# A conditioned two-layer transformer on one core: the order of a bias on GpSimd, the order of products at a stage's junction, and the slots of side work

## The chip, the core and the metric

The kernel runs on one core of a Trainium2 chip. A core has five engines with instruction streams of their own: TensorE (PE in the profile) multiplies matrices, VectorE (DVE) and GpSimd (POOL) do elementwise work and reductions, ScalarE (ACT) does elementwise functions, SyncE (SP) issues most of the DMA transfers. The metric is the time of one execution in microseconds (us). The kernel before took 1510.19, 1506.1 and 1509.9 us in three runs, a median of 1509.9 us.

## What is computed

x has 32 batches of 128 tokens with 512 features. Layer 0 acts on groups of four batches (512 tokens), with 16 heads; layer 1 acts on each batch's 128 tokens with a single head. Every batch also has a condition vector, from which the scales and shifts come.

```python
# layer 0 (h: the input; gamma, beta from the condition)
def sln(h):   # layer norm, then gamma * ln + beta
    mu, var = mean(h), mean((h - mu) ** 2)
    return gamma * ((h - mu) / sqrt(var + 1e-5) * ln_g + ln_b) + beta
q, k, v = split_heads(sln(h) @ Wqkv.T + bqkv)          # 16 heads of 32
out = softmax(q @ k.T) / sqrt(512) @ v
h1  = out @ Wp.T + bp + h
x   = sln(h1) + h1

# layer 1 (rmsnorm, then x * (1 + scale) + shift, both from the condition)
a = film(rmsnorm(x, norm1_w))
out = softmax((a @ q_w + q_b) @ (a @ k_w + k_b).T * 512 ** -0.5) @ (a @ v_w + v_b)
x = x + out @ proj_w + proj_b
m = film(rmsnorm(x, norm2_w))
x = x + gelu(m @ mlp_w1 + mlp_b1) @ mlp_w2 + mlp_b2     # 512 -> 2048 -> 512, exact gelu
```

## The kernel before

**Precision.** A factor is held as two parts, high (rounded to the matmul's fp32r type) and low (what is left). A product is the sum of three matmuls, high by high, high by low and low by high (mm3, L148). So wherever a factor is made there are an ACT cast for the high part and a subtraction for the low part, on VectorE or POOL.

**Order.** Nearly everything lies in two scheduled blocks in which PE, VectorE, ACT and POOL execute in the order of the program text; only SP's DMA queue is put in order by a scheduler. So the order of calls in the Python text is the order of each engine's queue: an instruction that waits holds back everything behind it on its engine. A product's instructions go to PE where `run(...)` stands; what follows it (`done`, an add or a cast) goes to its engine's queue at that place too. PSUM tiles for products have two buffers (mm_tile), so a product can begin only when what was in the tile two before has been read.

**Stages.** After a prologue, **loop one** (L1252 to L1320) has 32 steps s, a chunk of four heads of a group in each: energies, maxima, exponentials and heads_out of step s, the query and key products of step s+1, the layer norm of a later batch (`new`, class Turned), and the output projection of a batch whose heads are done (`end`, class End). An End loads x again (tile xe), adds the projection's bias on POOL (bias, L610), adds the product on VectorE (add, L625), takes the second sln's statistics (first: L296 to L301, the power on POOL L308, L639, L640 on POOL) and ends in second (L644 and a store). A Turned has the steps stats (VectorE L296 to L301 or L306, then the power -0.5 on POOL, L308, whose result is rn), norm (VectorE L374 in layer 0; L372 and L377 in layer 1), halves (ACT L386 and a transposing DMA), merge (VectorE L395), rest (ACT L412, L421) and low (L425, on POOL in layer 1).

The **junction** (L1331 to L1351) leads from layer 0 to layer 1. It is a list of eleven products of twelve matmuls each: K[1..3], the remaining keys of layer 1's group 0 (K[0] stands in loop one's last step); the numbers 0 to 3, the last four Ends, each with its bias on POOL before and its add behind, but with first and second put off to layer 1; and V[0..3], the values. Between them a Pipeline makes the normalised batches of the next group; at u=2 the low part (POOL L425) of the first of them is made.

**Layer 1's attention** (L1360 to L1400) runs over g = 0 to 6. A g scores and softmaxes group g (scores1, softmax1 with L756 on POOL and L759 to L762 on VectorE) and then has eight slots u. A slot runs one key or value product of group g+1 (V has its low part on VectorE, L123); beside it stand the division of the softmax (divided1, L775 and L776) at u=0, its transposes (turn1, tile psaT) at u=1, and the output products of group g (class Out: a load of xe, a bias on POOL L798 at u=2 to 5, product and add L805 at u=3 to 6). The put-off Ends have first at u=2 and second at u=4 of g=0 to 3.

Two kinds of MLP work are spread over these slots. **Tokens** are the first eight batches' second norm (Turned(2, b)): `at` names the slot (g, u) at which each begins with stats; its load comes two slots earlier, norm and halves one slot later, merge and rest six later, and rest ends in a store (hTd). **Columns** (L872) are the four columns i of the first half MLP's right-hand factors x, u, v, y: each loads two stored tokens (b = i and 4 + i), forms sums on VectorE (L890 to L893), high parts on ACT (heads) and low parts (tails, L909) one slot later, x and u on POOL, v and y on VectorE. Before, sums stand at u = 1, 2, 4, 6 of g=6 and a column is loaded one slot ahead.

The passage **g=7** (L1403 to L1425) has no next group; the first seven MLP products, hidden(0, 0), are put between the last scores, transposes and output products. Then **layer2** runs the MLP four times (n = 0 to 3), with columns for n = 1 to 3 inside.

Of the kernel before, what the change touches and what calls it, by code (L numbers as in the profile page):

```python
# [22 lines left out]
G = 4  # L23
NG = B // G
# [17 lines left out]
def cond_seq_kernel(ctx: ExitStack, tc, x, condT, wcond, w0, w1, wk1, wm1, wm2, cols, rows, out):  # L42
    nc = tc.nc
# [822 lines left out]
    def a_load(n, h):  # L866

        t = w_tile(f"A{n}{'hl'[h]}").rearrange("p c f -> p (c f)")[:, : NA * 2 * P]
        load(t.bitcast(FP), ad[n % FH, h])
        At.setdefault(n, []).append(t.rearrange("p (c k f) -> p c k f", c=NA, k=2))  # L870

    class Columns:  # L872
# [9 lines left out]
        def sums(self):  # L882
            n, i = self.n, self.i
            if i == 0:
                Bt[n] = [w_pair(f"B{n}{nm}") for nm in "xuv"]
                t = w_tile(f"B{n}y")
                Bt[n].append((t[:, :2], t[:, 2:]))
            r1, r2 = self.r
            t = d_tile(f"T{n}_{i}", FP, (P, 2 * KC, P))
            nc.vector.tensor_tensor(t[:, 0:2], r2[:, :2], r1[:, :2], ALU.subtract)  # L890
            nc.vector.tensor_tensor(t[:, 2:4], r2[:, 2:], r2[:, :2], ALU.subtract)
            nc.vector.tensor_tensor(t[:, 4:6], r2[:, 2:], t[:, 0:2], ALU.subtract)
            nc.vector.tensor_tensor(t[:, 6:8], t[:, 4:6], r1[:, 2:], ALU.subtract)  # L893
            self.parts = [
                (*(p[:, :, ts(i, P)] for p in pair), src, eng)
                for pair, src, eng in zip(
                    Bt[n],
                    (r1, t[:, :4], t[:, 4:], r2[:, 2:]),
                    (nc.gpsimd, nc.gpsimd, nc.vector, nc.vector),
                )  # L900
            ]

# [346 lines left out]
    with tc.manual_schedule(engines=ordered):  # L1249
        new, end = coming(0), None  # L1250
        staged = None
        for s in range(STEPS):  # L1252
# [4 lines left out]
                ready = None  # L1257
            if ready:
                ready.merge()
            if end:  # L1260
                end.bias()
            run(q)
            if s == STEPS - 1:
                staged()
# [6 lines left out]
            if new:  # L1271
                new.stats()
                new.norm()
            if ready:
                ready.low()
            if end:
# [26 lines left out]
            if s == STEPS - 1:  # L1303
                K = keys1(0)
# [24 lines left out]
        for slot in (-11, -10):  # L1329
            pipe.made[slot] = begins[slot]()  # L1330
        V = values1(0)  # L1331
        products = [K[1], K[2], 0, K[3], 1, V[0], 2, V[1], 3, V[2], V[3]]
        for u, stream in enumerate(products):
            pipe.start(u - 11)
            if u == 1:
# [15 lines left out]
            pipe.end(u - 11)  # L1351


        at = [(1, 5), (2, 5), (3, 5), (4, 1), (4, 5), (5, 1), (5, 3), (5, 5)]
        batches = [0, 1, 4, 5, 2, 6, 3, 7]
        columns, COLUMNS = {}, (1, 2, 4, 6)
        tokens = Pipeline(
            {2 * G * g + u: lambda b=b: Turned(2, b) for (g, u), b in zip(at, batches)}
        )
        for g in range(NG - 1):  # L1360
# [4 lines left out]
            for u in range(2 * G):  # L1365
                slot = 2 * G * g + u
                for line in (pipe, tokens):
                    line.start(slot)
                if u - 1 in columns:
                    columns[u - 1].tails()  # L1370
                if u in columns:
                    columns[u].sums()
                if 0 < u <= G:
                    outs.append(Out(g * G + u - 1))
                late = ends[g] if g < G else None
# [14 lines left out]
                    run(outs[u - 3].stream())  # L1390
                for line in (pipe, tokens):
                    line.end(slot)
                if u in columns:
                    columns[u].heads()
                if g == NG - 2:
                    if u + 1 in COLUMNS:
                        columns[u + 1] = Columns(0, COLUMNS.index(u + 1))
                    if u == 6:
                        for h in range(2):
                            a_load(0, h)  # L1400


        g = NG - 1  # L1403
# [8 lines left out]
        for j in range(3):  # L1412
            run(products[j])
        divided1(g)
        run(products[3])
        turn1(g)
        for o in outs:
            o.bias()
        run(products[4])
        for f in (0, FH):  # L1420
            wb_piece(f)
        for i, o in enumerate(outs):
            run(o.stream())
            if i < 2:
                run(products[5 + i])  # L1425
        row2 = load(r_tile("row2"), rows[R_B2].partition_broadcast(P))
        for q in (1, 3):
            wb_load(q)
# [74 lines left out]
```

## Time and profile before

The profile is of one execution on the chip, recorded by the hardware profiler.

| what | us |
|---|---|
| median of three runs | 1509.9 |
| the profiled execution | 1510.46 |
| its span in the trace | 1508.5 |
| loop one, 32 steps | 54 to 597 |
| junction, first key product to layer 1's first scores | 592.72 to 626.97 |
| layer 1, starts of g = 0 to 6 | 626.97, 656.23, 685.72, 716.23, 746.75, 776.57, 805.23 |
| passage g=7 | 841.60 to 861.35 |
| MLP | to 1508 |

The mean clock granted to TensorE was 0.993 of full speed. How to read it: times in the trace are microseconds from the span's start, and an instruction is named by its line and its output tile. The span is the time between the first and the last record; the execution is 2.0 us longer. A busy time counts the time in which an instruction is under way on its engine, including time in which it is held back while it runs. Before each instruction the trace gives the engine's idle time and the engine that ended it. Stages overlap, as the other engines work ahead of or behind TensorE; the boundaries in the table are TensorE's.

### The profile page before, as it was taken

Reading aid. Unit: us, or ns where it says so; the run is one execution under the profiler, and the core shown is the slowest. Engines: PE = TensorE matmul, PEld = TensorE weight load, DVE = VectorE, ACT = ScalarE, POOL = GpSimd, SP = SyncE. Lnnn points to the kernel's source line nnn. Section 1 sums busy time; section 2 is a strip of 40 time slices with the busy share of each in tenths; the row PEclk is TensorE's granted clock in tenths of the full one; section 3 lists DMA queues with packets and bytes.
Section 4 is the critical chain, followed back from the end, with each engine's and each line's share of the span. In section 5 each row is a group of like instructions: output and inputs, shape, how many; then the busy total and the mean of one; then the engine's idle time right before and its main releaser. Section 6 shows DMA issues by size and latency. Waiting matters only on the chain.

```text
span 1508.5 us, 25450 instructions
## 1 busy us (share of the span) xinstructions
PE 1478.3 (98%) x9612; PEld 1155.3 (77%) x9612; DVE 1008.4 (67%) x1793; ACT 760.5 (50%) x1415; POOL 499.5 (33%) x440
## 2 busy tenths in 40 slices
PE   8999999999999999999999899999999999999998
PEld 3767776777777766787887788888888888888887
DVE  4656777777777667889997776665557555754342
ACT  1455655566555444666786354535454345523331
POOL 1213554445453243466555422230014000340000
PEclk9999999999999999999999999999999999999999
DMA  8245465664655335788885877937776666934550
GB/s 312 85 151 157 125 198 176 188 190 134 178 152 175 111 115 178 193 209 225 233 214 173 356 238 236 307 132 209 225 266 208 194 203 219 326 122 134 184 173 29
DMA packets 226578, 287.85 MB, mean 191 GB/s; under 512 B 107252, under 2 KB 138100, under 8 KB 224024
## 3 DMA queue, kind: packets, MB, share of 16 engines
q1 hardware_dynamic: 225448, 278.89, 59.8%
q10 hardware_dynamic: 1008, 7.34, 1.4%
q8 instruction: 75, 1.23, 0.3%
q14 instruction: 47, 0.39, 0.1%
HBM read 194.23 MB, written 72.55 MB: 177 GB/s over the span
## 4 chain that ended last, share of the span: by engine, by line
PE 81%; DVE 11%; ACT 3%; issue 2%; POOL 1%; DMA 1%; SPq 0%; POOLq 0%; DVEq 0%; ACTq 0%
PE acc L981 23%; PE psh L157 20%; PE psk L157 6%; PE psv L157 5%; PE psq L157 5%; PE psp L157 5%; PE psV L157 2%; PE pse L526 2%; PE pst L561 2%; PE pso L581 2%; PE pss L586 2%; PE psT L157 1%; DVE tn L395 1%; PE pss L747 1%; DVE stn L296 1%
## 5 line engine op out<-in xcount | busy, mean ns | idle before, releaser
L308 POOL TENSOR_TENSOR rn<-vn,neghalf 128x1 f32<-128x1 f32 x96 | 61.6, 642 | 438.9 <-DVE vn L306 336.6
L386 ACT COPY tn<-x 128x1024 uint16<-128x1024 uint16 x90 | 94.0, 1045 | 60.5 <-DVE x L372 48.4
L919 ACT ACTIVATE c<-c,col 128x512 f32<-128x512 f32 x64 | 46.4, 725 | 141.2 <-DVE c L944 86.0
L538 DVE TENSOR_REDUCE nm<-pse 128x4 f32<-128x512 f32 x128 | 79.4, 682 | 19.4 <-PE pse L526 19.4
L997 POOL TENSOR_TENSOR xe<-xe,row 128x512 f32<-128x512 f32 x32 | 46.5, 1484 | 123.8 <-DMA xe<-xs 123.7
L934 DVE TENSOR_TENSOR c<-psh,ca 128x512 f32<-128x512 f32 x32 | 22.1, 692 | 89.9 <-PE psh L157 84.3
L395 DVE COPY tn<-tn 128x1024 uint16<-128x1024 uint16 x90 | 77.0, 855 | 1.0 <-DMA tn<-tn 1.0
L644 DVE SCALAR_TENSOR_TENSOR xe<-te,re,xe 128x512 f32<-128x512 f32 x28 | 41.1, 1467 | 47.4 <-POOL xe L640 47.4
L296 DVE BATCH_NORM_STATS2 stn<-x 128x6 f32<-128x512 f32 x96 | 65.4, 682 | 5.3 <-DMA x<-in_x 5.2
L568 ACT ACTIVATE e<-pst 128x512 f32<-128x512 f32 x128 | 65.8, 599 | 2.6 <-PE pst L561 2.5
L412 ACT ACTIVATE tn<-tn,mods 128x128 f32<-128x128 f32 x128 | 52.5, 481 | 19.0 <-DVE tn L395 19.0
L308 POOL TENSOR_TENSOR re<-ve,neghalf 128x1 f32<-128x1 f32 x32 | 30.9, 966 | 88.7 <-DVE ve L301 88.7
L372 DVE TENSOR_SCALAR x<-x,rn 128x512 f32<-128x512 f32 x64 | 52.9, 827 | 10.1 <-POOL rn L308 9.0
L610 POOL TENSOR_TENSOR xe<-xe,row 128x512 f32<-128x512 f32 x32 | 42.3, 1323 | 47.7 <-DMA xe<-in_x 46.8
L509 ACT ACTIVATE qk<-psq,col 128x512 f32<-128x512 f32 x32 | 22.1, 690 | 69.7 <-PE psq L157 63.5
L947 DVE TENSOR_TENSOR ca<-psh,ca 128x512 f32<-128x512 f32 x32 | 22.1, 691 | 41.5 <-PE psh L157 41.5
L561 PE MATMUL pst<-qk 32*128 32x128 f32 x1024 | 46.2, 295 | 0.0
L798 POOL TENSOR_TENSOR xe<-xe,row 128x512 f32<-128x512 f32 x32 | 45.8, 1444 | 1.1 <-DMA xe<-xs 1.1
L919 ACT ACTIVATE cb<-cb,col 128x512 f32<-128x512 f32 x32 | 23.2, 725 | 43.1 <-DVE cb L948 43.1
L526 PEld LDWEIGHTS pse<-qk 32*128 32x128 f32 x1024 | 32.1, 186 | 14.2 <-issue 12.7
L412 ACT ACTIVATE tn<-tn,mod 128x128 f32<-128x128 f32 x104 | 42.9, 485 | 0.0
L593 DVE TENSOR_TENSOR pss<-pss,rs 128x512 f32<-128x512 f32 x32 | 22.3, 697 | 29.9 <-ACT rs L592 29.8
(1388 smaller groups left out, 4846.5 us busy)
## 6 DMA issues: line engine op xcount, KB each, us to landing
mod<-mod SPq DMA_DIRECT2D x34, 512.0 KB, 5.4
x<-xs SPq DMA_DIRECT2D x64, 256.0 KB, 3.8
xe<-xs SPq DMA_DIRECT2D x64, 256.0 KB, 3.2
ur<-ud SPq DMA_DIRECT2D x64, 256.0 KB, 4.2
xs<-xe SPq DMA_DIRECT2D x60, 256.0 KB, 2.6
x<-in_x SPq DMA_DIRECT2D x32, 256.0 KB, 3.8
xe<-in_x SPq DMA_DIRECT2D x32, 256.0 KB, 4.3
scw<-scw SPq DMA_DIRECT2D x32, 256.0 KB, 4.7
```

What stands on the lines that cost most here:

```text
L157: nc.tensor.matmul(st["ps"], *calls[j], start=(j == 0), stop=(j == n - 1))
L296: nc.vector.bn_stats(st, t)
L308: nc.gpsimd.tensor_tensor(r, v, neghalf, ALU.pow)
L386: nc.scalar.copy(halves.rearrange("p (e d) -> p e d", e=2), X.bitcast(U16).rearrange("p (d e) -> p e d", e=2),)
L395: nc.vector.tensor_copy(self.a.bitcast(U16).rearrange("p (f e) -> p e f", e=2), self.t.bitcast(U16).rearrange("p (e f) -> p e f", e=2),)
L412: nc.scalar.activation(dst[:, c], self.a[:, ts(c, P)], AF.Identity, bias=m[:, q + B : q + B + 1], scale=m[:, q : q + 1],)
L526: nc.tensor.matmul(banks[r][:, ts(i, P)], q[32 * r : 32 * r + 32, ts(i, P)], k[32 * r : 32 * r + 32, ts(i, P)], start=True, stop=True,)
L538: nc.vector.tensor_reduce(nm[:, r], chunks(banks[r]), AX.X, ALU.max, negate=True)
L561: nc.tensor.matmul(banks[r][:, ts(i, P)], k[rr, ts(i, P)], q[rr, ts(i, P)], start=False, stop=True,)
L568: nc.scalar.activation(e, banks[r], AF.Exp)
L919: nc.scalar.activation(t[nm], t[nm], AF.Gelu, bias=col[:, C_B1 + f : C_B1 + f + 1], scale=1.0)
L981: nc.tensor.matmul(accs[i], u[pa][:, ts(i, P)], wb[f // 4][pb][:, f % 4, :], start=(first and j == 0), stop=(last and j == len(PARTS) - 1),)
```

## The change

Six edits, none of which adds or removes arithmetic. The number of TensorE instructions is the same; 32 subtractions pass from POOL to VectorE.

1. All four low parts of a column (L909) are VectorE's.
2. In loop one the bias of an End (POOL, L610) is queued behind the layer norm of the new batch, so behind its power (POOL, L308), and no longer before the query product.
3. In the junction, all three keys come first; then each End but the first has a V product before it.
4. Tokens begin at other slots: two in g=2 and g=3, one in g=5.
5. Columns have their sums at u = 0, 2, 4, 5 of g=6 and are loaded two slots ahead (the first one in g=5).
6. In g=7 hidden product 4 goes before the transposes (turn1), 5 before the output products, and 6 behind the first of them.

```diff
@@ Columns.sums
-                    (nc.gpsimd, nc.gpsimd, nc.vector, nc.vector),
+                    (nc.vector,) * 4,
@@ loop one
             if ready:
                 ready.merge()
-            if end:
-                end.bias()
             run(q)
...
             if new:
                 new.stats()
                 new.norm()
+            if end:
+                end.bias()
             if ready:
                 ready.low()
@@ junction
-        products = [K[1], K[2], 0, K[3], 1, V[0], 2, V[1], 3, V[2], V[3]]
+        products = [K[1], K[2], K[3], 0, V[0], 1, V[1], 2, V[2], 3, V[3]]
@@ layer 1
-        at = [(1, 5), (2, 5), (3, 5), (4, 1), (4, 5), (5, 1), (5, 3), (5, 5)]
+        at = [(1, 5), (2, 1), (2, 5), (3, 1), (3, 5), (4, 1), (4, 5), (5, 1)]
         batches = [0, 1, 4, 5, 2, 6, 3, 7]
-        columns, COLUMNS = {}, (1, 2, 4, 6)
+        columns, FIRST = {}, 2 * G * (NG - 2)
+        columns_at = {FIRST + u: i for i, u in enumerate((0, 2, 4, 5))}
...
-                if u - 1 in columns:
-                    columns[u - 1].tails()
-                if u in columns:
-                    columns[u].sums()
+                if slot - 1 in columns:
+                    columns[slot - 1].tails()
+                if slot in columns:
+                    columns[slot].sums()
...
-                if u in columns:
-                    columns[u].heads()
-                if g == NG - 2:
-                    if u + 1 in COLUMNS:
-                        columns[u + 1] = Columns(0, COLUMNS.index(u + 1))
-                    if u == 6:
-                        for h in range(2):
-                            a_load(0, h)
+                if slot in columns:
+                    columns[slot].heads()
+                if slot + 2 in columns_at:
+                    columns[slot + 2] = Columns(0, columns_at[slot + 2])
+                if slot == FIRST + 6:
+                    for h in range(2):
+                        a_load(0, h)
@@ passage g=7
         divided1(g)
-        run(products[3])
+        for j in (3, 4):
+            run(products[j])
         turn1(g)
         for o in outs:
             o.bias()
-        run(products[4])
+        run(products[5])
         for f in (0, FH):
             wb_piece(f)
         for i, o in enumerate(outs):
             run(o.stream())
-            if i < 2:
-                run(products[5 + i])
+            if i == 0:
+                run(products[6])
```

## The prediction

> **What bounds the kernel now.** First the page's busy times and its chain of waits:
>
> ```profile
> PE 1478.3 (98%) x9612; PEld 1155.3 (77%) x9612; DVE 1008.4 (67%) x1793; ACT 760.5 (50%) x1415; POOL 499.5 (33%) x440
> ...
> PE 81%; DVE 11%; ACT 3%; issue 2%; POOL 1%; DMA 1%; SPq 0%; POOLq 0%; DVEq 0%; ACTq 0%
> ```
>
> TensorE is busy nearly always and the change leaves its 9612 matmuls alone; only the time in which it waits, or runs with a cut clock, can move. Then busy time by stage (start:end and length, then busy time of each engine with its instructions, granted clock, DMA share, GB/s): loop one, junction, layer-one groups g=2 to 6, the passage to the MLP (g=7), the MLP.
>
> ```profile
> 54.00:597.00 543.00, 538.18 (x5431) 392.62 (x5430) 380.39 (x687) 304.29 (x573) 228.22 (x198) 1.00 0.51 153
> 597.00:627.00 30.00, 28.04 (x116) 22.38 (x115) 25.19 (x51) 17.04 (x32) 14.88 (x14) 0.94 0.80 225
> ...
> 685.70:716.20 30.50, 29.15 (x145) 24.08 (x144) 28.01 (x59) 21.79 (x47) 18.29 (x17) 1.00 0.86 233
> 716.20:746.75 30.55, 29.19 (x145) 24.07 (x144) 28.08 (x59) 21.82 (x47) 18.33 (x17) 1.00 0.90 244
> 746.75:776.60 29.85, 29.18 (x146) 24.11 (x145) 27.96 (x61) 23.32 (x49) 14.89 (x16) 1.00 0.89 215
> 776.60:805.20 28.60, 28.60 (x145) 24.13 (x144) 27.37 (x50) 24.34 (x53) 16.63 (x16) 1.00 0.79 208
> 805.20:841.60 36.40, 31.50 (x145) 26.07 (x144) 27.16 (x42) 19.49 (x46) 18.73 (x14) 0.91 0.53 179
> 841.60:861.40 19.80, 18.11 (x98) 15.12 (x97) 13.94 (x23) 8.48 (x18) 8.67 (x8) 1.00 1.01 408
> ```
>
> A group with the same products takes 28.6 us (g=5, no wait) to 36.4 us (g=6). Third, TensorE's waits from 597 us to 865 us:
>
> ```profile
> PE psV L157 <- DVE V L123: 8.4, 7, 4.9
> PE psp L157 <- DVE xe L625: 1.8, 1, 1.8
> PE psaT L785 <- DVE e L776: 1.7, 1, 1.7
> PE psV L157 <- DVE xe L625: 0.2, 1, 0.2
> ```
>
> All end at VectorE. The longest, 4.90 us at 832.70, is in g=6; twelve psV matmuls behind it take 440 ns instead of 227 (another 2.56 us). VectorE is late there because of how it shares with POOL, seen best in the timeline (start, duration, engine, line):
>
> ```profile
> 608.13 0.55 POOL L308 TENSOR_TENSOR rn<-vn,neghalf 128x1 f32<-128x1 f32 x1 [0.87 <-DVE vn L306]
> 608.65 1.28 POOL L610 TENSOR_TENSOR xe<-xe,row 128x512 f32<-128x512 f32 x1
> ```
> ```profile
> 608.72 1.50 DVE L372 TENSOR_SCALAR x<-x,rn 128x512 f32<-128x512 f32 x1 [0.73 <-POOL rn L308]
> ...
> 820.95 1.51 DVE L890 TENSOR_TENSOR T<-hT,hT 128x256 f32<-128x256 f32 x1
> ...
> 836.38 0.41 DVE L890 TENSOR_TENSOR T<-hT,hT 128x256 f32<-128x256 f32 x1
> ```
>
> Started 0.07 us after a POOL TENSOR_TENSOR, L372 lasts until that one's end plus 0.28 us; where POOL is quiet it takes 0.48 (at 599.33). L890 is 0.41 alone, 1.51 beside POOL.
>
> **Part 1: bias behind the power, loop one (28 steps).** It moves on POOL only. Before, POOL did bias L610 (1.29 us), then rn L308 (0.55), and L374 waited for rn:
>
> ```profile
> 201.70 1.29 POOL L610 TENSOR_TENSOR xe<-xe,row 128x512 f32<-128x512 f32 x1 [5.44 <-DMA xe<-in_x]
> 202.95 0.55 POOL L308 TENSOR_TENSOR rn<-vn,neghalf 128x1 f32<-128x1 f32 x1
> ```
>
> In this step vn was ready at 200.48 but rn stood behind a bias whose load had not landed; the step took 18.41 us against the 16.22 us of the quickest. After, rn goes at once. What hides it otherwise: x L374 feeds ACT's L386, which stands before the exponentials; they are late for TensorE only if L386 starts late by more than ACT's own queue (L421) and TensorE's key product cover.
> The price: the bias now starts as rn ends, L374 0.07 us after it, just the picture at 608.65. L374's 26 records show 0.55 us and none overlaps POOL, so its rows price the lock at nothing; L372, the same operation, says 1.5. The Trainium skill ("SBUF — State Buffer", Who interferes with whom) says that VectorE and GpSimd share a port pair as an exclusive lock, that tensor_scalar in its fast mode wants it, and that who issues first blocks the other fully; that speaks against this part. I went through the steps with both. Without a lock: gains 2.0 at 201.70, 1.4 at 236.55, 0.9 at 304.01, smaller ones elsewhere, together +5. With it (L374 ends 1.63 us after the bias starts): +2.0, +0.4 and +0.15 in three steps, where the bias lands late; −0.25 in each of six steps with an early load, 0.57 together lost in three more, 0 where TensorE's key product ends later anyway; and in the last step POOL's n_0l L425 comes 0.7 later, for which TensorE already waits. Sum 2.55 − 2.07 − 0.7 = **−0.2 us**. I take the lock, by L372's row; ends −6 (the early-load loss in all steps) and +5.
>
> **Part 2: junction.** Eleven products of twelve matmuls at 227 ns, 2.72 us each, need 30.0 us; they took 34.25 (592.72 to 626.97), as V[0] and End 2 wait for the adds L625 of End 0 and End 1 (two PSUM buffers serve Ends and V) and the clock was cut: psp 343 ns after a wait of 1.80. Now K[3] precedes End 0, and each End needs the add of the previous one with one V product (2.72 us) between. End 0 finishes at 603.74, V[0] at 606.46. Its bias now stands on POOL behind n_4l (605.90 to 607.2, bound to ACT's L421) and the next rn: 607.8 to 609.0, add to 609.75. So TensorE stalls 3.3 us at End 1. The later two Ends stall 0.4 and 1.7 by the same count, soft, taken at half. Cut clock: "TensorE: Matmul & The Clock Gate" (Part 1) puts the drop at half rate after an idle window of some 3.4 us, which would leave a 3.3 us stall without one; but here 1.80 cost 1.4 us and 4.90 cost 2.56, so I take 1.8 by the rows. 3.3 + 1.05 + 1.8 = 6.15 against 4.2: **−2.0 us**; ends −5 and +2 (End 0's bias before n_4l in time).
>
> **Part 3: token slots.** A token is VectorE stats (1.25 us), norm L372 (0.48, 1.3 blocked), merge L395 (0.75, 1.45 blocked), a POOL rn, ACT 1.04 + 1.65, a load, a transpose and a store on SP's queue (DMA share up by some 0.09). Of stats and merges, g=2 and g=3 go from one each to two each, g=4 keeps two, g=5 goes from three and two to one and two, g=6 loses two merges. g=5 has no wait to give back. g=2 and g=3 have the fullest VectorE, as the put-off Ends (L639, L644) run there, and wait already (1.11 + 0.25 us for V L123 in each). One token adds 2.5 to 4.0 us to 28.0 busy in a stage that TensorE alone would do in 28.66; VectorE's present idle 2.5 us takes part. I take −0.7, −1.7, and −0.5 carried into g=4: **−2.9 us**; ends 0 and −8.
>
> **Part 4: columns in g=6, lower parts on VectorE.** Eight POOL L909 leave (the ones blocking the L890 row), VectorE gets eight of 0.68: 5.4 us. A column is then 4 x 0.42 + 3 x 0.68 + 0.42 = 4.1 us, four of them 16.6, without the blocked 1.5s and the two merges. The 4.90 wait and its 2.56 of cut clock can go: at most +7.5. But POOL, freed, runs the eight biases L798 (1.28 each, their loads landed by 812; before they stood behind L909) from about 806.5 to 817, and there VectorE now does sums of column 0, four small operations that cost 1.5 each beside POOL, ahead of the division L775/L776 that TensorE's psaT needs (814.25 before, no wait): some 3.4 us of stall and 0.8 of clock. **+3.3 us**; ends 0 and +7.5.
>
> **Part 5: g=7.** Product 4 before turn1 covers the 1.69 us wait of psaT for e L776. But ACT now does that product chain's gelu (0.73) and cast (0.62), which wait for VectorE, before it copies aT for the output products: some 2.0 us. **−0.3 us**; ends −2 and +1.
> MLP: 2 x 0.68 more on VectorE for a column, under products that take 642.02 of 646.60 us; if that cover were gone, 12 x 1.36 = 16 us. Taken 0.
>
> **Sum**: −0.2 − 2.0 − 2.9 + 3.3 − 0.3 = −2.1. The profiled execution took 1510.46 us (span 1508.5, 2.0 around it); 1510.46 + 2.1 = 1512.6. The median of the runs shown is 1509.9, 0.6 lower, within their spread (1506.1 to 1510.19); I keep **1512.6**. A measurement of this kernel can tell 0.3%, 4.5 us, from no change.
>
> **Rivals.**
> - A, as forecast: the g=6 stall goes in part, junction and tokens take it back. 1512.6, own range 1508 to 1517. Chance 0.45.
> - B, faster: the lock doesn't bite where POOL moved (L374 stays 0.55, the L798s don't meet column 0). Then +5, −2.0, −2.9, +7.5, −0.3 = 7.3 us: 1503. For it: 26 clear L374; against: every overlapped row of L372, L890 and L909. Chance 0.20.
> - C, slower: VectorE becomes the bound in g=2 and g=3. It decides from the point where busy time plus the 2.5 us of idle that its own waits impose passes what the stage has, 30.5; with a token at its blocked price of 4.0, 32 + 2.5 = 34.5, or 4.0 longer in each, 8 in place of 2.9: 1517.7, and 1521 if the junction also goes to its end. For it: DMA share 0.86 to 0.90 there already. Against: g=4 and g=5 carry two and three tokens at no cost, though without put-off Ends. Chance 0.35.
> - That the slots don't move is excluded: they are written out by hand.
>
> **How the numbers follow.** A gives 0.02 faster, 0.37 same, 0.06 slower; B 0.18 faster, 0.02 same; C 0.02 same, 0.33 slower: 0.20, 0.41, 0.39. The range goes to B with three us more (1500) and to C with the junction's end (1522).
>
> **What would show it.** Right: L374 near 1.5 us in early-load steps; a psp wait of about 3 us near 606.5; psV waits over 2 us in g=2 and g=3; in g=6 no psV wait near 5, but a psaT wait near 814 with L890 at 1.5. Wrong: L374 at 0.55 throughout; End 1 unstalled; g=2 and g=3 still 30.5 us long; psaT unwaited, then g=6 comes near 29 us and the kernel is faster.

## The result and the profile after

The changed kernel takes 1517.57 us (median of six runs, 1513.31 to 1519.19) against 1509.29 us for the kernel before; the ratio is 1.0057, with a 95% interval from 1.0037 to 1.0077. It is slower by about 8 us. The profiled execution is the quickest of the six: 1513.31 us, span 1511.5.

The page's busy times and chain of waits of the changed kernel:

```profile
PE 1478.3 (98%) x9612; PEld 1155.0 (76%) x9612; DVE 1022.2 (68%) x1825; ACT 762.5 (50%) x1415; POOL 449.6 (30%) x408
...
PE 77%; DVE 13%; DMA 3%; issue 3%; ACT 2%; POOL 2%; SPq 0%; POOLq 0%; DVEq 0%; ACTq 0%
```

TensorE's busy time is unchanged to the digit. POOL lost 49.9 us, VectorE gained only 13.8, and the chain now runs through DMAs for 3% of the span (1% before). So the difference is waiting, and the stages say where. Starts are read from TensorE's first instruction of each stage:

| stage | before, us | after, us | difference |
|---|---|---|---|
| start to step 1's energies | 77.44 | 73.80 | −3.64 |
| loop one, steps 1 to 30 | 500.73 | 497.53 | −3.20 |
| step 31 and junction, to layer 1's first scores | 48.80 | 51.90 | +3.10 |
| g = 0, 1 | 58.75 | 58.79 | +0.04 |
| g = 2 | 30.51 | 31.04 | +0.53 |
| g = 3 | 30.52 | 35.71 | +5.19 |
| g = 4, 5 | 58.48 | 58.07 | −0.41 |
| g = 6 | 36.37 | 33.30 | −3.07 |
| g = 7 | 19.75 | 19.15 | −0.60 |
| MLP | 647.15 | 652.21 | +5.06 |

The first row has nothing to do with the change. Nothing that it moves runs there, and what varies lies ahead of step 0, which takes 23.1 to 23.2 us from its energies to step 1's in every profiled execution. Over the profiled executions of all kernels of this study the row comes in two kinds: 73.6 to 73.8 us (three executions, one of them a kernel whose only edit is in g=7) and 76.6 to 79.3 us (the others). The windows of the first 54 us show TensorE with another granted clock, first before, then after (the clock is the number behind POOL):

```profile
0.00:54.00 54.00, 46.15 (x134) 23.33 (x134) 31.55 (x58) 15.77 (x28) 13.83 (x22) 0.91 0.71 262
```
```profile
0.00:54.00 54.00, 46.33 (x152) 23.95 (x153) 31.02 (x59) 16.96 (x30) 14.38 (x22) 0.97 0.73 262
```

So spans can't be compared as they stand. Without that row the changed kernel is 6.6 us longer in the traces; the medians are 8.3 us apart, and what makes the other 1.7 no trace shows. Below, differences of stages are taken from traces, and verdicts from the timed runs.

TensorE's waits from 596 us to the end, in the changed kernel:

```profile
PE psV L157 <- DVE V L123: 7.7, 6, 4.8
PE psp L157 <- DVE xe L625: 3.8, 2, 3.2
PE psh L157 <- DVE ca L951: 3.3, 1, 3.3
PE psaT L785 <- ACT B0y L905: 2.8, 1, 2.8
PE pso L157 <- ACT aT L122: 0.9, 1, 0.9
```

Each of the first four long waits is one row of the table: 4.8 in g=3 (before, the 4.9 was in g=6), 3.2 in the junction, 3.3 in the MLP, 2.8 in g=6. The busy times of those stages (junction with step 31, g=3, g=6, MLP) show the granted clock (the number behind POOL's) cut behind them in the first three, 0.95 to 0.97. Over the long MLP the mean hides it; the last row is the 5 us behind the MLP's wait, at 0.66:

```profile
571.33:623.23 51.90, 46.91 (x286) 35.15 (x286) 36.74 (x75) 26.81 (x49) 19.63 (x20) 0.97 0.53 151
...
713.06:748.77 35.71, 30.88 (x145) 25.13 (x144) 31.16 (x68) 25.53 (x54) 19.51 (x19) 0.95 0.91 245
...
806.84:840.14 33.30, 30.49 (x146) 25.25 (x145) 26.53 (x46) 16.26 (x37) 11.82 (x11) 0.95 0.47 151
...
859.29:1511.50 652.21, 644.97 (x2833) 532.14 (x2831) 367.25 (x630) 266.30 (x449) 76.02 (x70) 1.00 0.63 201
...
880.39:885.39 5.00, 5.00 (x15) 3.95 (x16) 2.69 (x8) 4.06 (x8) 0.22 (x1) 0.66 1.04 408
```

**Junction.** The timeline of POOL, VectorE and TensorE at End 1 reads as the prediction wrote it, all some 6 us earlier, as the start and loop one were shorter:

```profile
599.72 1.30 POOL L425 TENSOR_TENSOR n_4l<-n_4f,n_4h 128x512 fp32r<-128x512 f32 x1 [2.04 <-ACT n_4h L421]
601.36 0.55 POOL L308 TENSOR_TENSOR rn<-vn,neghalf 128x1 f32<-128x1 f32 x1 [0.35 <-DVE vn L306]
601.88 1.26 POOL L610 TENSOR_TENSOR xe<-xe,row 128x512 f32<-128x512 f32 x1
```
```profile
603.18 0.69 DVE L625 TENSOR_TENSOR xe<-psp,xe 128x512 f32<-128x512 f32 x1 [1.96 <-POOL xe L610]
```
```profile
603.92 0.50 PE L157 MATMUL psp<-w0ph,o7h 128*128 128x512 f32 x1 [3.22 <-DVE xe L625]
```

End 0's bias stands on POOL behind n_4l and a power; its add waits for it, and TensorE, which finished V[0], waits for the add.

**g=3.** TensorE's wait of 4.83 us, which ended at 740.90, is for the low part of V on VectorE. First VectorE and POOL ahead of it:

```profile
733.01 1.29 POOL L640 TENSOR_TENSOR xl<-xl,mod 128x512 f32<-128x512 f32 x1
734.27 3.42 POOL L798 TENSOR_TENSOR xe<-xe,row 128x512 f32<-128x512 f32 x2
```
```profile
733.07 1.79 DVE L377 SCALAR_TENSOR_TENSOR scw<-x,scw 128x512 f32<-128x512 f32 x1
...
734.78 1.82 DVE L395 COPY tn<-tn 128x1024 uint16<-128x1024 uint16 x1
...
740.16 0.68 DVE L123 TENSOR_TENSOR V<-psV,V 128x512 fp32r<-128x512 f32 x1
```

L377 and a merge L395 are held 1.1 us each by POOL. But the kernel before has the same:

```profile
731.99 1.79 DVE L377 SCALAR_TENSOR_TENSOR scw<-x,scw 128x512 f32<-128x512 f32 x1
...
733.71 1.83 DVE L395 COPY tn<-tn 128x1024 uint16<-128x1024 uint16 x1
...
739.17 0.68 DVE L123 TENSOR_TENSOR V<-psV,V 128x512 fp32r<-128x512 f32 x1
```

What differs is when this sequence comes: V's low part starts 27.1 us behind the group's first scores instead of 22.9. Nearly all of these 4.2 us are there already at aT, the transposed probabilities, whose cast on ACT and low part on VectorE come 3.85 us later in the group than before:

```profile
722.40 0.41 SPq L417 DMA_DIRECT2D hTd<-tn  x1
```
```profile
727.37 0.59 ACT L122 CAST aT<-psaT 128x512 fp32r<-128x512 f32 x1 [3.09 <-DMA hTd<-tn]
```
```profile
727.99 0.69 DVE L123 TENSOR_TENSOR aT<-psaT,aT 128x512 fp32r<-128x512 f32 x1 [3.04 <-ACT aT L122]
```

ACT stands still for 3.09 us until a token's store (hTd, issued at 722.40, landed at 727.29) is done, and VectorE stands still behind it. TensorE had finished the transposes in psaT before 722.9. In the kernel's text aT and the token's tile come from one pool of buffers (`d_tile`), so the cast waits for the store that still reads its buffer: at the new slots the store falls just ahead of the cast. Another 0.65 us come from a token's merge that now stands ahead of the softmax's maxima on VectorE. From aT on VectorE has no gap, before and after alike. So VectorE is busy for 31.16 us of this group, where TensorE's products take 28.6, but what made the group longer is mainly how late that stretch begins. In g=2, with as many tokens, aT doesn't wait, and the group is only 0.5 us longer than before.

**g=6.** The column's sums stand on VectorE ahead of the division, and POOL's biases L798 run from 807.89 to 817.1:

```profile
812.94 0.17 DVE L762 TENSOR_SCALAR nm<-nm 128x4 f32<-128x4 f32 x1
813.02 1.55 DVE L890 TENSOR_TENSOR T<-hT,hT 128x256 f32<-128x256 f32 x1
814.49 1.52 DVE L891 TENSOR_TENSOR T<-hT 128x256 f32<-128x256 f32 x1
815.93 1.48 DVE L892 TENSOR_TENSOR T<-hT,T 128x256 f32<-128x256 f32 x1
817.45 0.42 DVE L893 TENSOR_TENSOR T<-T,hT 128x256 f32<-128x256 f32 x1
817.79 0.17 DVE L775 RECIPROCAL inv<-total 128x4 f32<-128x4 f32 x1
```

Three sums take 1.5 us and the fourth, after POOL is done, 0.42. The division follows, so psaT starts at 818.83, 2.81 us late. (The table of waits names ACT's L905, which ended last before 818.83 by a hair; the division's L776, begun at 818.00, is the operand.)

**MLP.** VectorE in the changed kernel:

```profile
871.60 0.68 DVE L948 TENSOR_TENSOR cb<-psh,cb 128x512 f32<-128x512 f32 x1
879.03 0.74 DVE L395 COPY tn<-tn 128x1024 uint16<-128x1024 uint16 x1 [6.76 <-DMA tn<-tn]
879.66 0.68 DVE L951 TENSOR_TENSOR ca<-psh,ca 128x512 f32<-128x512 f32 x1
```

The merge of the MLP's first token waits 6.76 us for its transposing DMA; behind it stands L951, which frees the PSUM tile that TensorE needs next. TensorE waits 3.27 us, and the first twelve matmuls behind it, seven of them at 427 ns instead of 227, cost another 1.7: together the 5 us of the table. Before, the same merge waited 1.05 us, and TensorE not at all.

### The profile page after: what moved, and what is told of

The parts are those of the page before. It is cut to its first block, busy times and chain, and to the rows that moved or that the text cites. A ratio compares the mean times of both kernels' runs of the same rounds, so it can differ in the third digit from the quotient of the medians.

```text
span 1511.5 us, 25444 instructions
## 1 busy us (share of the span) xinstructions
PE 1478.3 (98%) x9612; PEld 1155.0 (76%) x9612; DVE 1022.2 (68%) x1825; ACT 762.5 (50%) x1415; POOL 449.6 (30%) x408
## 4 chain that ended last, share of the span: by engine, by line
PE 77%; DVE 13%; DMA 3%; issue 3%; ACT 2%; POOL 2%; SPq 0%; POOLq 0%; DVEq 0%; ACTq 0%
PE acc L981 23%; PE psh L157 19%; PE psv L157 5%; PE psk L157 5%; PE psq L157 5%; PE psp L157 4%; PE psV L157 2%; PE pso L581 2%; PE pse L526 2%; PE pst L561 2%; PE pss L586 2%; PE psT L157 2%; DVE tn L395 2%; DVE stn L296 1%; DVE x L372 1%
## 5 line engine op out<-in xcount | busy, mean ns | idle before, releaser
L308 POOL TENSOR_TENSOR rn<-vn,neghalf 128x1 f32<-128x1 f32 x96 | 61.8, 644 | 559.6 <-DVE vn L306 402.9
L997 POOL TENSOR_TENSOR xe<-xe,row 128x512 f32<-128x512 f32 x32 | 44.5, 1415 | 190.7 <-DMA xe<-xs 176.6
L395 DVE COPY tn<-tn 128x1024 uint16<-128x1024 uint16 x90 | 79.1, 879 | 6.8 <-DMA tn<-tn 6.8
L934 DVE TENSOR_TENSOR c<-psh,ca 128x512 f32<-128x512 f32 x32 | 22.1, 692 | 89.2 <-PE psh L157 83.6
L412 ACT ACTIVATE tn<-tn,mods 128x128 f32<-128x128 f32 x128 | 52.5, 481 | 16.8 <-DVE tn L395 16.8
L372 DVE TENSOR_SCALAR x<-x,rn 128x512 f32<-128x512 f32 x64 | 53.6, 838 | 9.2 <-POOL rn L308 8.6
L509 ACT ACTIVATE qk<-psq,col 128x512 f32<-128x512 f32 x32 | 22.1, 690 | 69.6 <-PE psq L157 63.5
L308 POOL TENSOR_TENSOR re<-ve,neghalf 128x1 f32<-128x1 f32 x32 | 30.9, 967 | 82.3 <-DVE ve L301 81.5
L947 DVE TENSOR_TENSOR ca<-psh,ca 128x512 f32<-128x512 f32 x32 | 22.1, 691 | 41.6 <-PE psh L157 41.6
L798 POOL TENSOR_TENSOR xe<-xe,row 128x512 f32<-128x512 f32 x32 | 45.1, 1425 | 16.7 <-DMA xe<-xs 16.7
L374 DVE TENSOR_SCALAR x<-x,mvn,rn 128x512 f32<-128x512 f32 x26 | 35.1, 1348 | 17.7 <-POOL rn L308 17.7
L919 ACT ACTIVATE cb<-cb,col 128x512 f32<-128x512 f32 x32 | 23.2, 725 | 42.7 <-DVE cb L948 42.7
L1001 DVE TENSOR_TENSOR xe<-acc,xe 128x512 f32<-128x512 f32 x32 | 21.1, 688 | 32.5 <-PE acc L981 32.5
```

What stands on the lines that cost most here:

```text
L308: nc.gpsimd.tensor_tensor(r, v, neghalf, ALU.pow)
L372: nc.vector.tensor_scalar(X, X, r, None, ALU.mult)
L395: nc.vector.tensor_copy(self.a.bitcast(U16).rearrange("p (f e) -> p e f", e=2), self.t.bitcast(U16).rearrange("p (e f) -> p e f", e=2),)
L412: nc.scalar.activation(dst[:, c], self.a[:, ts(c, P)], AF.Identity, bias=m[:, q + B : q + B + 1], scale=m[:, q : q + 1],)
L919: nc.scalar.activation(t[nm], t[nm], AF.Gelu, bias=col[:, C_B1 + f : C_B1 + f + 1], scale=1.0)
```

## Experiments

Each is timed against the kernel before. First the parts alone, then sums of parts, then the causes.

**The bias behind the norm, alone.**

```diff
-            if end:
-                end.bias()
             run(q)
...
                 new.norm()
+            if end:
+                end.bias()
```

> Only the bias's place in loop one. The profiles before and after put loop one from step 1's energies to step 31's energies at 500.7 and 497.5 us, so the bias theory says: 3 us of gain in the time (ratio 0.998), with L374 at about 1.35 us on average instead of 0.55 and the gain in the two steps where the bias waited for its load. If the shared port costs as much as it saves, as the prediction had it, the ratio is 1.000. Step 0 took 23.2 us before and 18.8 after; if that comes from this part, step 0 is near 18.8 here as well; if it is a chance of the execution, it need not be.

Ratio 0.9983 (0.9974 to 0.9992): 2.6 us faster by the medians (1506.46 against 1509.09). Steps 1 to 30 take 498.43 us, 2.3 less. L374 is held in 22 of its 26 records; this is its row (count, minimum/median/maximum in ns, first and last start), first before, then here:

```profile
L374 DVE TENSOR_SCALAR x<-x,mvn,rn x26: 545/546/548, 68.1 to 483.8; 128x512 f32<-128x512 f32 x26
```
```profile
L374 DVE TENSOR_SCALAR x<-x,mvn,rn x26: 545/1494/1505, 64.3 to 477.4; 128x512 f32<-128x512 f32 x26
```

So the lock is there in full and the part gains all the same. The two steps whose bias waited for its load fall from 18.41 and 18.50 to 17.51 and 17.03; both vary from execution to execution (17.5 to 18.5 and 18.1 to 18.8 in those with the bias in its old place, 16.7 to 17.5 and 16.9 to 18.1 in those with the new one and no gap). The six steps with an early load, for which a loss of 0.25 each was counted, gain 0.1 to 0.3. One of them shows why, first before, then here:

```profile
164.45 1.29 POOL L610 TENSOR_TENSOR xe<-xe,row 128x512 f32<-128x512 f32 x1 [1.17 <-DMA xe<-in_x]
164.56 1.21 DVE L540 TENSOR_TENSOR nmx<-nm,nmx 128x16 f32<-128x16 f32 x1
...
168.07 0.55 DVE L374 TENSOR_SCALAR x<-x,mvn,rn 128x512 f32<-128x512 f32 x1 [0.66 <-POOL rn L308]
```
```profile
160.59 0.18 DVE L540 TENSOR_TENSOR nmx<-nm,nmx 128x16 f32<-128x16 f32 x1
...
163.08 1.50 DVE L374 TENSOR_SCALAR x<-x,mvn,rn 128x512 f32<-128x512 f32 x1 [0.66 <-POOL rn L308]
```

An early bias had a lock of its own before: it held a small operation ahead of the layer norm (L539 or L540, 0.87 to 1.25 us instead of 0.17) in these six steps and in no other of steps 4 to 26. Without it L374 starts 1.0 us earlier in its step (6.41 us behind the step's energies instead of 7.43), which pays for the 0.95 that it is held. Three steps with a late load, 12, 13 and 15, lose 0.72, 0.20 and 0.38 (step 12 varies by 0.4 without the part), and the last two 0.4 and 0.5. Step 0 takes 23.14 us here and 23.17 both before and after, so the 18.8 us that the expectation gives was misread; the start took 73.64 us here, but a later run without this part shows the same.

**The junction's order, alone.**

```diff
-        products = [K[1], K[2], 0, K[3], 1, V[0], 2, V[1], 3, V[2], V[3]]
+        products = [K[1], K[2], K[3], 0, V[0], 1, V[1], 2, V[2], 3, V[3]]
```

> Only the order of the junction's products. Theory: TensorE stalls about 3.2 us at End 1 (psp waiting for xe L625) and the stage from step 31's energies to layer 1's first scores takes 51.9 us instead of 48.8, so 3 us slower (ratio 1.002). Rival: the stall comes from the bias of loop one arriving late in the last step; then the junction alone costs nothing.

Ratio 1.0006 (0.9998 to 1.0014). In the trace step 31 and the junction take 51.31 us instead of 48.80, with one psp wait of 3.5 us for xe L625: the stall is the junction's own and not the late bias's. In the timed runs its cost can't be told from nothing.

**The token slots, alone.**

```diff
-        at = [(1, 5), (2, 5), (3, 5), (4, 1), (4, 5), (5, 1), (5, 3), (5, 5)]
+        at = [(1, 5), (2, 1), (2, 5), (3, 1), (3, 5), (4, 1), (4, 5), (5, 1)]
```

> Only the token slots. Theory that VectorE's room in g=2 and g=3 is used up: g=3 takes about 35.7 us instead of 30.5 with a psV wait near 4.8 us, g=5 gains nothing; g=6 loses its two merges and gains up to 3 us, so 2 to 6 us slower (ratio 1.001 to 1.004). Rival: g=3's stall in the changed kernel comes from its phase after the junction, not from the tokens: then g=2 and g=3 stay at 30.5.

Ratio 1.0014 (1.0007 to 1.0022). g=2 takes 31.05, g=3 35.04, g=6 31.70 us: 4.5 us lost in g=3 come back in g=6, where two merges are gone. The rival falls as the whole cause: g=3 is long without the other parts. But the phase matters for the size: ACT's cast of aT waits 1.2 us for the token's store here and TensorE 3.38 us for V, against 3.1 and 4.8 in the changed kernel. All six kernels with the new token slots show that wait, of 1.2 to 3.1 us, and none of the eight others does. A buffer of its own for aT was not tried.

**Lower parts on VectorE, alone.**

```diff
-                    (nc.gpsimd, nc.gpsimd, nc.vector, nc.vector),
+                    (nc.vector,) * 4,
```

> Only the lower parts on VectorE. Theory: in g=6 the psV wait of 4.9 us for V L123 shrinks, as L890 and L891 are no longer held by POOL's L909, but VectorE has 5.4 us more: g=6 between 33 and 36 us (36.4 before), the MLP unchanged, so up to 3 us faster (ratio 0.998 to 1.000). Rival: the MLP's extra stall in the changed kernel (3.3 us at psh behind L395) comes from here; then the kernel is 1 to 3 us slower, with that wait in the trace.

Ratio 0.9972 (0.9962 to 0.9983), 4.5 us faster by the medians. g=6 falls to 29.16 us, more than expected; this is its window:

```profile
806.07:835.23 29.16, 28.73 (x145) 24.16 (x144) 23.98 (x46) 19.57 (x46) 11.89 (x11) 1.00 0.61 191
```

VectorE has eight subtractions more and is busy 23.98 us instead of 27.16, as little holds it: three of its four L890 take 0.40 to 0.42 us. The 4.90 us wait and the cut clock are gone entirely. The MLP is 1.4 us longer, with 1.1 us of psh waiting for L951, so part of the rival is there too.

**Lower parts, column slots and token slots together.** The edit is the change's hunks for columns and for `at`.

> The lower parts on VectorE, the columns' new slots and the token slots together; loop one, junction and g=7 as before. Theory: the lower parts alone took g=6 from 36.4 to 29.2 us and tokens alone to 31.7; both take the same stall away, so it can be saved once. The new slots put sums of column 0 before the division: psaT waits about 2.8 us, with cut clock g=6 is near 33 us as in the changed kernel, and g=3 near 35. So this is 3 to 8 us slower than the lower parts alone (ratio 1.000 to 1.003). Rival: g=6's loss in the changed kernel comes from part 2 or the junction (a shift of phase); then g=6 is near 29 us here.

Ratio 1.0009 (0.9999 to 1.0020), 0.0037 above the lower parts alone. g=3 35.35, g=6 31.70, MLP 651.08 us; psaT waits 2.8 us.

**The order in g=7, alone.**

```diff
         divided1(g)
-        run(products[3])
+        for j in (3, 4):
+            run(products[j])
         turn1(g)
...
-        run(products[4])
+        run(products[5])
...
-            if i < 2:
-                run(products[5 + i])
+            if i == 0:
+                run(products[6])
```

> Only the order of products in g=7. Theory A: the extra 5 us of the changed kernel's MLP (psh waiting 3.3 us for L951, which stands behind the merge L395 that waits 6.8 us for its transposing DMA) come from this part, as it lets TensorE leave g=7 earlier while the same loads must pass: then the MLP is 3 to 5 us longer here and the ratio 1.001 to 1.003. Theory B: they come from the time that g=6 gains, which starts the MLP's loads and stores closer together; then the MLP is unchanged here (647 us) and the ratio 0.999 to 1.000.

Ratio 1.0018 (1.0007 to 1.0028). g=7 itself takes 22.83 us instead of 19.75: psaT's wait is gone, but the first output product waits 2.1 us for aT, and the clock is at 0.93 there. The MLP is unchanged (647.03). That alone doesn't refute theory A, as TensorE leaves g=7 later here and not earlier; two other runs do: the MLP loses 3.9 us without this part (the run above, with the lower parts and both kinds of slots) and 0.2 with it and the columns' old slots (below).

**The bias and the lower parts.** Both edits above, nothing else.

> The bias's place and the lower parts on VectorE, nothing else. If the two gains (2.6 us and 4.2 us, from medians) don't touch each other, the ratio is 0.9955 (1502.3 us); if the shorter way to the MLP is given back there (psh behind the merge that waits for its DMA), 0.997.

Ratio 0.9977 (0.9965 to 0.9988): less than hoped. In the profiled execution both gains are whole (steps 1 to 30 498.18, g=6 29.12, MLP 648.36); in the timed runs, from 1499.73 to 1508.96, they are not.

**The change without the columns' slots.** Sums at u = 1, 2, 4, 6 and loads one slot ahead, as before.

> The changed kernel with the columns' sums at u = 1, 2, 4, 6 and loaded one slot ahead, as before. Theory: no psaT wait in g=6, which comes down from 33.3 to about 29 us, 4 us faster than the changed kernel (1513.5 us); g=3 stays near 35.7 and the junction at 51.9. If the MLP's extra wait has its cause in the columns' new slots (their earlier loads), it goes too, and the kernel is near 1509 us. Rival: another wait takes its place in g=6 (the columns' loads come late or L123 stands behind column work) and the time stays at 1517.

Ratio 1.0009 (0.9999 to 1.0019), from 1.0057: the slots are the dearest part of the change, and these two intervals lie apart. g=6 takes 28.91 us and the MLP 647.37, without a wait at L951.

**The change with later merges in the MLP's first pass.**

```diff
+        lag = 2 if n == 0 else 1
...
-                if j == 5 and fp:
-                    state[fp - 1].merge()
-                if j == 6 and fp:
-                    state[fp - 1].rest()
+                if j == 5 and fp >= lag:
+                    state[fp - lag].merge()
+                if j == 6 and fp >= lag:
+                    state[fp - lag].rest()
...
-            state[FH - 1].merge()
-            state[FH - 1].rest()
+            for fp in range(FH - lag, FH):
+                state[fp].merge()
+                state[fp].rest()
```

> The changed kernel with the merge and rest of each token of the MLP's first pass (n=0) one round of seven products later; nothing else. Theory: the 3.3 us wait of psh for L951 in the changed kernel is only the merge L395 standing in VectorE's queue while its transposing DMA waits behind some 11 MB of loads; with the merge later the wait goes, the MLP falls from 652.2 to 647 us and the time by 4 to 5 us (about 1512.5). Rival: TensorE is short of the loads themselves there (the A tiles); then another psh wait, for a DMA, takes the place and the time stays near 1517.

1513.49 us, ratio 1.0033 (1.0020 to 1.0047), from 1.0057, with intervals that overlap; the trace is clear. The MLP takes 647.74 us and psh no longer waits. The MLP's loss was this merge in VectorE's queue.

Why does its DMA land too late? The traces give, in us behind TensorE's first accumulation of the MLP, when the transposing DMA was issued and when it landed, and beside it how long TensorE waited for L951 (A0l is one of the MLP's first loads):

| kernel | A0l issued | transposing DMA issued | landed | TensorE's wait |
|---|---|---|---|---|
| before | −23.5 | 5.8 | 14.6 | 0 |
| change without column slots | −22.8 | 5.7 | 16.0 | 0 |
| tokens | −22.1 | 7.0 | 16.3 | 0 |
| lower parts | −21.4 | 10.1 | 17.5 | 1.1 |
| bias, lower parts | −21.4 | 10.4 | 17.7 | 0.8 |
| lower parts, slots, tokens | −20.2 | 10.1 | 18.8 | 2.3 |
| change, division first (below) | −22.3 | 8.4 | 18.8 | 2.3 |
| change | −21.0 | 8.6 | 19.7 | 3.3 |
| change, later merges | −21.0 | 8.4 | 19.7 | 0 |

Where the DMA lands by 16.3 us TensorE doesn't wait, behind that it waits, and broadly the more the later it lands. In the last row it lands as late as in the change, and nothing waits for it. Two things make up the 5.1 us between the first row and the change. TensorE is 2.5 us sooner behind the loads, and the transposing DMA itself takes longer, 11.1 us from issue to landing instead of 8.8:

```profile
867.18 5.74 SPq L390 DMA_TRANSPOSE tn<-tn  x1
```
```profile
867.87 3.98 SPq L390 DMA_TRANSPOSE tn<-tn  x1
```

In both kernels the DMA engines are busy all the way (a share of 1.01 and 0.99 from A0l's issue to this one's), and SP waits with this DMA for the landing of an earlier load, A2l. In the changed kernel A0l is issued 3.9 us after its sister A0h instead of 0.45: between them in SP's queue stands a store that waits for VectorE's L805 until 837.84. The four kernels with the columns' new slots have 3.0 to 3.9 us there, all others at most 0.52. That this order is what makes the DMA late is argued, not tried; and as the rows of the lower parts show, a shorter way to the MLP makes it late too, though less.

**The bias, the lower parts and the later merges.**

> The bias's place and the lower parts on VectorE, with the merges of the MLP's first pass one round later. Both waits of the MLP there (0.8 us for L951, 1.0 us for the DMA of A0l) were small, so 1 to 2 us less than without the later merges: MLP 647 us instead of 648.4, ratio to before about 0.996 to 0.997.

1502.87 us, ratio 0.9957 (0.9943 to 0.9971): 6.5 us faster than the kernel before, and the lowest median of the study. In the profiled executions the merges make no difference (MLP 648.23 against 648.36). The timed ratio is lower than without them (0.9977), but the two intervals overlap a little, so that the later merges help here is likely and not shown.

**A gap between the norm and the bias.** The edit against the bias alone:

```diff
                 new.norm()
             if end:
+                if new:
+                    nc.gpsimd.tensor_tensor(gap, new.X[:, :1], neghalf, ALU.add)
                 end.bias()
```

> The bias behind the norm as in the run with the bias alone, but POOL first reads one column of the normalised tile, so that the bias can't start before L374 is done. Theory of the shared port: L374 is 0.55 us again instead of 1.49 and steps 11 to 15 (16.8 to 16.9 us, where L386 waited for L374) come down to 16.3, and the last two steps from 17.3 and 17.4 to 16.9: loop one is 2 to 4 us shorter than with the bias alone (498.4 to about 495.5), ratio to before 0.996. Rival: those steps are longer for another reason (when loads land, what POOL does next); then L374 is 0.55 and the steps stay.

Ratio 1.0006 (0.9997 to 1.0015): the gain of the bias part is gone. L374 is back at 0.55 us and the last two steps at 16.94 and 16.88, as the theory has it; but steps 11, 13 and 15 take 17.8 us, longer than with the lock (16.8). One of them, with the lock (the bias alone):

```profile
281.08 1.49 DVE L374 TENSOR_SCALAR x<-x,mvn,rn 128x512 f32<-128x512 f32 x1 [0.66 <-POOL rn L308]
282.49 0.68 DVE L425 TENSOR_TENSOR n_16l<-tn,n_16h 128x512 fp32r<-128x512 f32 x1
283.10 0.68 DVE L625 TENSOR_TENSOR xe<-psp,xe 128x512 f32<-128x512 f32 x1
```

and with the gap:

```profile
287.91 0.55 DVE L374 TENSOR_SCALAR x<-x,mvn,rn 128x512 f32<-128x512 f32 x1 [0.66 <-POOL rn L308]
288.65 0.69 DVE L425 TENSOR_TENSOR n_16l<-tn,n_16h 128x512 fp32r<-128x512 f32 x1 [0.19 <-ACT n_16h L421]
290.52 0.69 DVE L625 TENSOR_TENSOR xe<-psp,xe 128x512 f32<-128x512 f32 x1 [1.19 <-POOL xe L610]
```

From L374's start to the add L625 it is 2.02 us with the lock and 2.61 with the gap: now L625 waits for the bias (1.81 us itself, as L425 holds it), and behind L625 hang the second norm and the next step's maxima on VectorE. In the steps that take 16.2 us (5 to 7 and 16 to 25) L374 is 0.95 us shorter with the gap and the step stays 16.2: there the lock is off the path. The lock costs less than what it takes to avoid it in this way. A bias on another engine wasn't tried.

**The division before the sums, in the changed kernel.**

```diff
-                if slot in columns:
+                if slot in columns and u:
                     columns[slot].sums()
...
                 if u == 0:
                     divided1(g)
+                    if slot in columns:
+                        columns[slot].sums()
```

> The changed kernel with one thing moved: at u=0 of g=6 the sums of column 0 are queued on VectorE behind the division (L775, L776) instead of ahead of it. The sums still meet POOL's biases L798 and still take 1.5 us each. Theory: TensorE's wait of 2.8 us at psaT and the cut clock behind it come from the sums standing ahead of the division; both go, g=6 falls from 33.3 to about 29.5 us, and the time by up to 4 us (1513.5), or less where the MLP's wait for its DMA grows by what g=6 gains. Rival: the division is late anyway, as POOL's biases hold the softmax's own small operations (L761 took 1.22 us there) and ACT is behind with the column's casts L905: then psaT still waits over 2 us.

1516.21 us, ratio 1.0035 (1.0024 to 1.0047), an interval that overlaps with the changed kernel's; the trace decides here. g=6 falls from 33.30 to 29.64 us, and psaT waits 0.2 us:

```profile
819.70 1.12 DVE L776 TENSOR_TENSOR e<-e,inv 128x512 f32<-128x512 f32 x1
820.74 1.50 DVE L890 TENSOR_TENSOR T<-hT,hT 128x256 f32<-128x256 f32 x1
822.16 0.41 DVE L891 TENSOR_TENSOR T<-hT 128x256 f32<-128x256 f32 x1
```

The sums meet less of POOL's biases as well. Of the 3.7 us, g=7 takes back 1.2; the MLP keeps its loss (651.10).

| kernel | ratio | steps 1–30 | junction | g=3 | g=6 | g=7 | MLP |
|---|---|---|---|---|---|---|---|
| before | 1 | 500.73 | 48.80 | 30.52 | 36.37 | 19.75 | 647.15 |
| bias | 0.9983 | 498.43 | 49.33 | 30.51 | 36.20 | 19.87 | 646.08 |
| junction | 1.0006 | 500.93 | 51.31 | 30.53 | 35.88 | 19.93 | 646.11 |
| tokens | 1.0014 | 500.91 | 47.81 | 35.04 | 31.70 | 20.53 | 647.09 |
| lower parts | 0.9972 | 500.46 | 48.63 | 30.52 | 29.16 | 19.58 | 648.59 |
| lower parts, slots, tokens | 1.0009 | 500.16 | 48.65 | 35.35 | 31.70 | 18.36 | 651.08 |
| g=7 | 1.0018 | 500.86 | 47.65 | 30.50 | 35.88 | 22.83 | 647.03 |
| change without column slots | 1.0009 | 498.34 | 53.41 | 35.96 | 28.91 | 19.55 | 647.37 |
| change | 1.0057 | 497.53 | 51.90 | 35.71 | 33.30 | 19.15 | 652.21 |

The token slots' trace gains nothing and loses nothing in sum where the timed runs show 2 us. That lies in which executions were profiled: the one of before took 1510.46 us, 1.4 above the median of its runs there, the one of the token slots 1510.27, 0.7 below its own. A difference of 2 us between two traces is no finding by itself.

## Why the prediction held, and where it did not

The time lies in the range, and the direction is the one forecast; the size is not: 2.1 us were counted, 8 came. That the time lies in the range is luck in part, as the two dearest terms, g=3 and the MLP, have causes that the prediction did not have. By its steps:

- **Loop one: −0.2 us counted, 3.2 us gained (2.3 alone).** The lock came as the row of L372 said (1494 ns), which the 26 clear rows of L374 did not show. The loss laid on it was mis-sized: the six steps with an early load were to lose 0.25 each and gained 0.1 to 0.3 each. The prediction added the new lock on L374 and left rn's time as it was. It overlooked that the early bias held L539 or L540 before, 0.7 to 1.1 us more in just these steps, so that L374 starts that much earlier without it: one lock took another's place. What was lost lay elsewhere, 1.3 in steps 12, 13 and 15 and 0.9 in the last two (0.57 in three steps was counted). The last step of all, in the junction's row of the table, was sized about right: for the later POOL L425 psT waits 1.14 us instead of 0.32, and 0.7 was counted.
- **Junction: −2.0 counted, −3.1 measured with step 31, −2.5 alone.** The stall at End 1 was put at 3.3 us and is 3.22, by the very instructions named. The later two Ends stalled 0.54 us together and not the 1.05 taken. The cut clock came out as taken, with 371 ns on average for the twelve psp matmuls behind the wait (1.7 us; 1.8 taken), but that is luck: behind the same wait of 3.21 us the run with the division first shows no cut at all.
- **Tokens: −2.9 counted, −5.3 measured** (g=2 to g=4). The mechanism counted on, VectorE's room, fits g=2, which lost 0.5 (0.7 counted) with a psV wait of 1.65 us, not the 2 forecast; g=4 gained 0.4 where a loss of 0.5 was carried over. The 5.2 us of g=3 are mainly something else, which neither the forecast nor rival C has: 3.1 us in which ACT waits for a token's store to free a buffer, and VectorE behind it, with the cut clock on top. Tokens alone get the loss back in g=6, which the prediction gave to the columns.
- **Columns in g=6: +3.3 counted, +3.07 measured,** with the psaT wait where it was put. But this sum hides two things. The lower parts alone bring 7.2 us there and the token slots alone 4.7; both take from one stall, the 4.90 us and the 2.56 of cut clock behind it (with the tokens alone 2.84 and no cut are left), so it is gained once. (The L890 at 820.95 that the prediction lays to an L909 was held by a bias L798, on POOL from 820.71; the L891 behind it by an L909.) And the new slots then cost 4.4 (33.30 against 28.91 without them).
- **g=7: −0.3 counted, +0.6 measured;** alone it costs 3.1, by the wait for aT that was named (2.1 us).
- **MLP: taken 0, measured −5.06.** This is the term that failed. The prediction looked for added VectorE work under TensorE's products and found it covered. It did not ask what else stands in VectorE's queue there: the merge ahead of L951 waits for a transposing DMA, which lands 19.7 us behind the MLP's first accumulation instead of 14.6, half because TensorE comes sooner and half because the DMA comes later. Putting the merge one round later takes the loss away.

Together: 3.2 − 3.1 − 5.3 + 3.1 + 0.6 − 5.1 = −6.6 us, in the traces. The time forecast for rival C, 1517.7, is what was measured, but by chance: C has VectorE as the bound of g=2 and g=3, and no loss in the MLP.

## What to carry to other kernels

A stall that several edits relieve is gained once; measure each edit alone before adding them up: here two of the six edits gain 2.6 and 4.5 us alone, and the whole change loses 8. A tile's buffer can cost more than an engine's room: moving side work moved a store next to a cast that wanted its buffer. When a stage gets shorter, look at the first DMA-bound stretch behind it: what an in-order engine waits for there may land no sooner than before, or later, and everything queued behind that wait pays. And a contended port is priced by the path behind the blocked instruction, in the new place and in the old one: L374 nearly tripled in 22 steps and the loop still got faster, while a few blocked operations ahead of one division cost 3 us.

## What the runs showed of the hardware

- A VectorE tensor_scalar of 128x512 whose start falls 0.07 us behind that of a POOL tensor_tensor takes 1.49 us instead of 0.55, in 22 of 26 cases; small operations are held as long (L540 of 128x16 1.21 us instead of 0.18, L761 of 128x4 1.22 instead of 0.16). In the other order POOL is the one held (L610 1.81 us instead of 1.28 behind L425). This is the exclusive lock of the Trainium skill ("SBUF — State Buffer", Who interferes with whom), also in its point that the order of issue decides.
- TensorE's granted clock can fall behind waits shorter than the idle window that the Trainium skill ("TensorE: Matmul & The Clock Gate", Part 1) gives, some 3.4 us, but need not. Over the 5 us behind the psp wait of the junction it is 0.66 in the changed kernel (wait 3.22 us, then seven matmuls at 427 ns instead of 227) and 1.00 in the run with the division first (3.21 us); behind the psaT wait of 2.81 us in g=6 0.66 in the changed kernel and 1.00 in the run with the lower parts, slots and tokens. In the 14 profiled executions, from 200 us on, it fell behind every wait of 3.38 us or more (to between 0.50 and 0.66), behind none of 1.3 to 1.7, and behind some of those between.
- With the same instructions in it, the start up to step 1's energies took 73.6 to 79.3 us from execution to execution, with a granted clock from 0.84 to 0.97 over its first 54 us. A difference of some microseconds between two spans can come from there.
